# A cross-attention block in float32 on one core: empty instructions in the stream of the matrix engine

## The chip, the cores and the metric

The kernel runs on one core of a Trainium2 chip. The core has five engines that run side by side, each with its own stream of instructions: TensorE (PE, matrix products), VectorE (DVE), ScalarE (ACT), GpSimd (POOL) and SyncE (SP, which here only starts transfers). Engines wait for each other through semaphores. The metric is the device time of one execution in microseconds (us), lower is better.

## The reference

The reference is one block of a transformer with attention from a sequence to a context. `x` and `ctx` are 128 sequences of 128 tokens with 256 features; there are 16 heads of 16 features; all is float32.

```python
q = (x @ Wq + bq);  k = (ctx @ Wk + bk);  v = (ctx @ Wv + bv)     # split into 16 heads
scores = einsum('bhqd,bhkd->bhqk', q, k) / sqrt(16)
scores = where(j < i, scores, -1e30);  attn = softmax(scores);  attn[:, :, 0, :] = 0
x1  = layer_norm(x + (attn @ v) @ Wo + bo, ln1_g, ln1_b)
out = layer_norm(x1 + relu(x1 @ W1 + b1) @ W2 + b2, ln2_g, ln2_b)  # W1: 256 x 1024
```

## The kernel before

The work is cut into 64 pairs of sequences, numbered p = 0 to 63. A pair has 256 tokens. All loops are unrolled in Python: the program has no branch in it, and each engine runs through one long list of instructions from first to last. The order on each engine is the order in which the calls are written, since the kernel asks for a manual schedule. A first part that is written out by hand and the functions `third`, `fourth` and `fifth` bring the pipeline up; `step(p)` for p = 5 to 63 is its steady part; `behind` and the lines from L1200 on empty it.

A step works on several pairs at once. On PE its order is:

1. `weigh(p - 2)` (L461): softmax weights times values, 96 matmuls of 32 columns (L471 and L481).
2. `scores_both(p)` (L347): queries times keys, 64 matmuls on 32 rows by 64 columns (L364).
3. `queries(p + 1)`, `attention_out(p - 2)`, `keys(p + 1)`, `values(p)` (L257, L500, L289): 32 matmuls that stream 256 columns.
4. `second_by_seven(p - 4)` (L771): the second product of the feed-forward part, written as seven products of half size in the manner of Strassen; each `product` (L778) has four matmuls in the program, and the seven go through L780. It starts with step 7.
5. `hidden(p - 3, ...)` (L676): the first product of the feed-forward part, 32 matmuls that stream 256 columns (L687).

A float32 matmul of the program stands in PE's stream as two matmuls with a weight load ahead of each (a transpose as one with one load), so the seven products are 56 matmuls and 56 weight loads. The counts above are those of the stream. A step of the stream holds 280 matmuls and 280 weight loads, and some instructions that only wait for a semaphore (EVENT_SEMAPHORE in the profile).

At the very start PE waits for an identity matrix that POOL makes (`ident`), runs twelve transposes of it whose result nobody reads (L833 to L835), then transposes the first context and input (`ptc` and `ptx`, L224, called from L840), and projects keys and queries (`pk` L859, `pq` L880). Scores, mask, softmax and the first use of the weights follow from these.

The other engines, in a step: DVE adds the mask (L378, L729), finds the maxima (L733, L740), sums the exponentials (L409), turns blocks (L424, L651); ACT computes exponentials (L748) and moves results out of PSUM (L268, L279, L299, L493, L693); POOL divides by the sums (L411) and adds the operands of the seven products (`combine_hidden`, L766 to L769); SP starts the transfers.

Of the kernel before, what the change touches and what calls it, by code (L numbers as in the profile page):

```python
# [13 lines left out]
P = 128  # L14
# [5 lines left out]
def tile_cross_attention_block(  # L20
# [22 lines left out]
    nc = tc.nc  # L43
# [6 lines left out]
    FC = DFF // P  # L50
# [116 lines left out]
    for part in (slice(0, HP), slice(HP, P)):  # L167
        nc.gpsimd.affine_select(
            out=neg[part, 1, :], in_=neg[part, 1, :], compare_op=ALU.is_gt, fill=NEG_INF,
# [10 lines left out]
    for e in range(2):  # L180
        nc.gpsimd.affine_select(
            out=half4[:, e, :], in_=half4[:, e, :], compare_op=ALU.is_ge, fill=0.0,
# [3 lines left out]
            out=half4[:, e, :], in_=half4[:, e, :], compare_op=ALU.is_ge, fill=0.0,  # L186
# [22 lines left out]

    def at_bank(i, name):  # L210
        return psum.tile([P, 512], F32, tag=f"b{i}", name=name)

    def bank(name):
        turns[0] += 1
        return at_bank(4 + turns[0] % 4, name)
# [47 lines left out]
    def queries(p):  # L263
        st = states[p]
        st["qT"] = proj.tile([P, KC, TP], F32, tag="qT", name=f"qT_{p}")
        pq = project(wq, st["xT"], at_bank(4, f"pq_{p}") if p > 3 else bank(f"pq_{p}"))
        for m in range(KC):
            nc.scalar.activation(  # L268
                st["qT"][:, m, :], pq[:, m * TP : (m + 1) * TP], AF.Identity,
                bias=bqs_c[:, m : m + 1], scale=QSCALE,  # L270
            )

    def keys(p):
        st = states[p]
        st["kT"] = proj.tile([P, KC, 2, TP], F32, tag="kT", name=f"kT_{p}")
        pk = project(wk, st["cT"], at_bank(0, f"pk_{p}") if p > 3 else bank(f"pk_{p}"))
        for m in range(KC):
            for e in range(2):
                nc.scalar.activation(  # L279
                    st["kT"][:, m, e, :], pk[:, m * TP : (m + 1) * TP], AF.Identity,  # L280
                    bias=bkh[:, m, e : e + 1], scale=half[:, e : e + 1],
                )
# [467 lines left out]
    wt = const.tile([P, 4, FC // 2, P], F32, tag="wt", name="wt")  # L750
# [20 lines left out]
    def second_by_seven(p):  # L771

        st = states[p]
        hT, hs = st["hT"], st["hS"]
        py = st["py"] = at_bank(6, f"py_{p}")
        pz = st["pz"] = at_bank(7, f"pz_{p}")

        def product(out, left, right):  # L778
            for k in range(FC // 2):
                nc.tensor.matmul(  # L780
                    out, left(k), right(k), start=(k == 0), stop=(k == FC // 2 - 1)
                )

        def raw(e, s):
            return lambda k: hT[:, 2 * k + e, s * P : (s + 1) * P]

        def weights(e, h):
            return lambda k: w2[:, 2 * k + e, h * P : (h + 1) * P]

        product(py[:, :P], raw(0, 0), weights(0, 0))  # L790
        product(pz[:, :P], raw(1, 0), weights(1, 0))
        product(pz[:, 2 * P : 3 * P], raw(1, 1), lambda k: wt[:, 3, k])
        product(py[:, 3 * P :], lambda k: hs[:, 0, k], lambda k: wt[:, 0, k])
        product(py[:, 2 * P : 3 * P], lambda k: hs[:, 2, k], lambda k: wt[:, 2, k])
        product(py[:, P : 2 * P], lambda k: hs[:, 1, k], lambda k: wt[:, 1, k])
        product(pz[:, P : 2 * P], lambda k: hs[:, 3, k], weights(1, 1))

    def sum_of_seven(p):

# [31 lines left out]
        nc.vector.tensor_tensor(st["t2"][:, s], py[:, :D], st["x1b"][:, s], ALU.add)  # L831

    warm = bank("warm")  # L833
    for i in range(12):
        nc.tensor.transpose(warm[:, i % 4 * P : (i % 4 + 1) * P], ident, ident)  # L835
    states[0] = {}
# [271 lines left out]
    def step(p):  # L1108
# [41 lines left out]
        if p > 6:  # L1150
            second_by_seven(p - 4)
        elif p == 6:
            second_half(2, 1)
# [26 lines left out]
    def behind(p):  # L1180

        weigh(p)
        context(p)
        combine_hidden(p - 2, BOTH)
        norm2(p - 3)
        second_by_seven(p - 2)
        attention_out(p)
        attention_sum(p)
        attention_stats(p)
        shift(p, 1)  # L1190
        residual1(p - 1)
        finish(p - 3)
        store(p - 3)
        sum_of_seven(p - 2)
        stats(p - 2, states[p - 2]["t2"], 2)
        scale_and_shift(p - 2)
        hidden(p - 1, range(FC), lambda f: norm1(p) if f == 0 else None)
        turn_x1(p)
# [5 lines left out]
    combine_hidden(p - 1, BOTH)  # L1204
    norm2(p - 2)
    second_by_seven(p - 1)
    residual1(p)
    finish(p - 2)
# [11 lines left out]
    for s in range(2):  # L1220
        py = at_bank(6 + s, f"py_last_{s}")
# [50 lines left out]
```

## Time and profile before

| | us |
|---|---|
| median of 3 runs | 1553.75 |
| lowest, highest | 1552.18, 1554.89 |
| the profiled execution | 1555.99 |
| its span, first to last instruction | 1554.0 |
| PE busy with matmuls in it | 1521.2 |
| PE busy with weight loads in it | 1363.3 |
| DVE, POOL, ACT busy in it | 1327.8, 1265.7, 1120.5 |

The profile is taken by the hardware from one execution. Its page gives the busy time of each engine, the span in slices, the DMA queues, the chain of work that ended last, and groups of instructions. The trace behind it is asked for more: the waits of an engine and what ended them, the instructions in order of time, or the busy time in windows that one chooses. In a row of the timeline stand the start, the length, the engine, the line of the kernel, the operation, the tile written and the tiles read, the shape and the count; in brackets the idle time before it and what ended that. "issue" means that the engine waited for nothing that the profile shows. PEld is the loading of weights, which goes on beside the matmuls. A row "PEldq EVENT_SEMAPHORE" is a wait that PE's sequencer handles; its three numbers are the shortest, the median and the longest in ns.

### The profile page before, as it was taken

The page shows a single profiled execution, that of the slowest core. Times are in us where ns is not written, and L with a number is a line of the kernel's source. Part 1 is how long each engine was busy: PE and PEld are TensorE (multiplying, and loading weights), DVE is VectorE, ACT ScalarE, POOL GpSimd, SP SyncE. Part 2 cuts the span into 40 slices and gives each one's busy share as a digit, 9 for nine tenths or more (in the row PEclk, how much of TensorE's full clock was granted, in tenths as well). Part 3 has the DMA queues.
Part 4 walks back from the last instruction along what each step waited for, and adds up shares of the span by engine and source line. Part 5 has one row for each costly group of instructions (what it writes and reads, how often), then busy time and mean ns, then how long its engine had stood idle before and what let it go on. Part 6 is the DMA issues. An engine that isn't in the chain of part 4 may idle for free.

```text
span 1554.0 us, 47426 instructions
## 1 busy us (share of the span) xinstructions
PE 1521.2 (98%) x17926; PEld 1363.3 (88%) x17926; DVE 1327.8 (85%) x2490; ACT 1120.5 (72%) x3391; POOL 1265.7 (81%) x1290
## 2 busy tenths in 40 slices
PE   8997999999999999999999999999999999999998
PEld 7786989989899889899899899899898899899887
DVE  7987889888889889889889889889889889888854
ACT  5656778777778768778778778678778677777742
POOL 6875888887888888888888888888888888888874
PEclk9999999999999999999999999999999999999999
DMA  8355655555566556556556566556565566554431
GB/s 196 83 120 120 143 134 134 136 132 136 137 138 142 131 134 140 138 134 144 121 138 146 132 140 138 128 136 148 131 139 130 131 138 149 133 136 120 107 91 48
DMA packets 415283, 204.21 MB, mean 131 GB/s; under 512 B 282448, under 2 KB 383056, under 8 KB 415056
## 3 DMA queue, kind: packets, MB, share of 16 engines
q1 hardware_dynamic: 413152, 200.13, 55.7%
q8 instruction: 142, 2.33, 0.7%
q10 hardware_dynamic: 1904, 1.06, 0.3%
q14 instruction: 85, 0.70, 0.1%
HBM read 70.26 MB, written 33.29 MB: 67 GB/s over the span
## 4 chain that ended last, share of the span: by engine, by line
PE 92%; DVE 3%; POOL 3%; issue 1%; ACT 1%; DMA 0%; POOLq 0%; DVEq 0%
PE ph L687 27%; PE py L780 13%; PE pz L780 10%; PE pq L257 8%; PE po L500 7%; PE pv L289 7%; PE pk L257 7%; PE pss L364 6%; PE pc L481 3%; PE pc L471 2%; POOL sm L411 1%; PE py L705 0%; DVE tb L424 0%; DVE sm L378 0%; POOL sd L521 0%
## 5 line engine op out<-in xcount | busy, mean ns | idle before, releaser
L687 PE MATMUL ph<-x1T,w 128*128 128x256 f32 x2048 | 454.0, 379 | 3.0 <-ACT kT L279 3.0
L687 PEld LDWEIGHTS ph<-x1T,w 128*128 128x128 f32 x2048 | 384.6, 190 | 53.9 <-ACT kT L279 3.4
L411 POOL TENSOR_TENSOR sm<-sm,rs 128x1024 f32<-128x1024 f32 x192 | 359.3, 1898 | 7.1 <-ACT hT L693 4.5
L693 ACT ACTIVATE hT<-ph,b1e_c 128x256 f32<-128x256 f32 x504 | 209.8, 468 | 188.3 <-PE ph L687 181.3
L748 ACT ACTIVATE sm<-pss,nmx 128x128 f32<-128x128 f32 x944 | 249.8, 415 | 132.4 <-DVE nmx L733 72.5
L748 ACT ACTIVATE sm<-sm,nmx 128x64 f32<-128x64 f32 x944 | 231.9, 334 | 5.1
L409 DVE TENSOR_REDUCE su<-sm 128x8 f32<-128x1024 f32 (+1 forms) x192 | 225.8, 1176 | 9.4 <-ACT sm L748 5.6
L378 DVE TENSOR_TENSOR sm<-pss,neg 128x256 f32<-128x256 f32 (+1 forms) x276 | 108.0, 433 | 133.0 <-PE pss L364 125.2
L424 DVE STREAM_TRANSPOSE tb<-sm 128x1024 f32<-128x1024 f32 x186 | 220.7, 1213 | 0.0
L520 POOL TENSOR_SCALAR ve<-mv 128x2 f32<-128x2 f32 x127 | 29.7, 234 | 212.4 <-DVE mv L514 212.0
L780 PE MATMUL py<-wt,hS 128*128 128x128 f32 x1440 | 172.0, 276 | 2.9 <-POOL hS L767 2.9
L780 PEld LDWEIGHTS py<-wt,hS 128*128 128x128 f32 x1440 | 166.4, 192 | 3.5 <-POOL hS L767 3.5
L733 DVE TENSOR_REDUCE nmx<-pss 128x4 f32<-128x512 f32 x236 | 150.5, 678 | 0.0
L257 PE MATMUL pq<-xT,wq 128*128 128x256 f32 x504 | 127.3, 396 | 4.9 <-DVE sm L378 4.9
L279 ACT ACTIVATE kT<-pk,bkh,half 128x256 f32<-128x256 f32 x252 | 120.3, 558 | 4.0 <-PE pk L257 4.0
L289 PE MATMUL pv<-wv,cT 128*128 128x256 f32 x512 | 121.1, 379 | 1.6 <-ACT sm L748 1.6
L500 PE MATMUL po<-wo,cxT 128*128 128x256 f32 x512 | 122.4, 382 | 0.0
L257 PE MATMUL pk<-cT,wk 128*128 128x256 f32 x504 | 119.2, 379 | 0.0
L257 PEld LDWEIGHTS pq<-xT,wq 128*128 128x128 f32 x504 | 91.7, 192 | 25.8 <-issue 9.4
L289 PEld LDWEIGHTS pv<-wv,cT 128*128 128x128 f32 x512 | 97.1, 190 | 15.1 <-ACT sm L748 2.0
L500 PEld LDWEIGHTS po<-wo,cxT 128*128 128x128 f32 x512 | 98.0, 192 | 14.0 <-ACT cxT L493 0.3
L257 PEld LDWEIGHTS pk<-cT,wk 128*128 128x128 f32 x504 | 95.7, 190 | 13.1 <-issue 0.2
(131 smaller groups left out, 2973.3 us busy)
## 6 DMA issues: line engine op xcount, KB each, us to landing
pT<-tb SPq DMA_DIRECT2D x984, 96.0 KB
x1t<-tbx SPq DMA_DIRECT2D x252, 64.0 KB
x1T<-x1t SPq DMA_DIRECT2D x63, 256.0 KB
out_dram<-t SPq DMA_DIRECT2D x63, 256.0 KB
xb<-in_x_dram SPq DMA_DIRECT2D x124, 128.0 KB
cb<-in_ctx_dram SPq DMA_DIRECT2D x124, 128.0 KB
x<-in_x_dram SPq DMA_DIRECT2D x31, 512.0 KB
w<-in_L_xattn_W_dram SPq DMA_DIRECT2D x2, 1024.0 KB
```

The source lines that it names most:

```text
L257: nc.tensor.matmul(ps[:, m * TP : (m + 1) * TP], w[:, k, m * P : (m + 1) * P], src[:, k, :], start=(k == 0), stop=(k == KC - 1),)
L279: nc.scalar.activation(st["kT"][:, m, e, :], pk[:, m * TP : (m + 1) * TP], AF.Identity, bias=bkh[:, m, e : e + 1], scale=half[:, e : e + 1],)
L289: nc.tensor.matmul(pv[:, s * D : (s + 1) * D], st["cT"][:, k, s * P : (s + 1) * P], wv[:, k, :], start=(k == 0), stop=(k == KC - 1),)
L409: nc.vector.tensor_reduce(su, sm[:, part, :], AX.X, ALU.add)
L411: nc.gpsimd.tensor_tensor(sm[:, part, :], sm[:, part, :], rs[:, :, None].to_broadcast([P, part.stop - part.start, n]), ALU.mult,)
L424: nc.vector.transpose(st["tb"][:, :, at : at + 256].rearrange("p j (n a) -> p n j a", a=32), st["sm", hi].rearrange("p h j -> p (h j)")[:, ...
L500: nc.tensor.matmul(po[:, s * D : (s + 1) * D], cxT[:, k, s, :], wo[:, k, :], start=(k == 0), stop=(k == KC - 1),)
L687: nc.tensor.matmul(ph[:, i * TP : (i + 1) * TP].rearrange("p (s i a) -> p s i a", s=2, a=32), w1[:, k, (f + i) * P : (f + i + 1) * P], st[ ...
L693: nc.scalar.activation(st["hT"][:, f + i, :], ph[:, i * TP : (i + 1) * TP], AF.Relu, bias=(b1e_c if p else b1_c)[:, f + i : f + i + 1], sc ...
L733: nc.vector.tensor_reduce(st["nmx", 1][:, 4 * r : 4 * r + 4], st["sps", 1][r].rearrange("p (n j) -> p n j", j=P), AX.X, ALU.max, negate=True,)
L748: nc.scalar.activation(sm[:, h, :], src, AF.Exp, bias=nmx[:, h : h + 1], scale=1.0)
L780: nc.tensor.matmul(out, left(k), right(k), start=(k == 0), stop=(k == FC // 2 - 1))
```

## The change

A new function puts empty instructions into PE's stream; they read nothing, write nothing and wait for nothing. In `second_by_seven`, each of the seven products gets one, behind its first matmul (`1 // 4 + (1 % 4 > k)` is one for k = 0 and none for k = 1 to 3). With these seven a step has 576 instructions on PE. 44 more stand at the start, ahead of the twelve transposes of `ident`. The seven products run 60 times (57 in the steps from p = 7 on, three while the pipeline empties), so 464 empty instructions are added. No other engine's list changes.

```diff
+    def empty(n):
+        for _ in range(n):
+            nc.tensor.nop(hint="pad", nofuse=True)
+
...
-        def product(out, left, right):
+        def product(out, left, right, after):
             for k in range(FC // 2):
                 nc.tensor.matmul(
                     out, left(k), right(k), start=(k == 0), stop=(k == FC // 2 - 1)
                 )
+                empty(after // (FC // 2) + (after % (FC // 2) > k))
...
-        product(py[:, :P], raw(0, 0), weights(0, 0))
+        product(py[:, :P], raw(0, 0), weights(0, 0), 1)
...
     warm = bank("warm")
+    empty(44)
     for i in range(12):
         nc.tensor.transpose(warm[:, i % 4 * P : (i % 4 + 1) * P], ident, ident)
```

The six other calls of `product` get the same last argument, 1.

More of the change, by code (lines that the diff above doesn't have):

```diff
@@ L788, in weights @@
             return lambda k: w2[:, 2 * k + e, h * P : (h + 1) * P]
-        product(py[:, :P], raw(0, 0), weights(0, 0))
[L791 to L796, printed above, removed]
+        product(py[:, :P], raw(0, 0), weights(0, 0), 1)
+        product(pz[:, :P], raw(1, 0), weights(1, 0), 1)
+        product(pz[:, 2 * P : 3 * P], raw(1, 1), lambda k: wt[:, 3, k], 1)
+        product(py[:, 3 * P :], lambda k: hs[:, 0, k], lambda k: wt[:, 0, k], 1)
+        product(py[:, 2 * P : 3 * P], lambda k: hs[:, 2, k], lambda k: wt[:, 2, k], 1)
+        product(py[:, P : 2 * P], lambda k: hs[:, 1, k], lambda k: wt[:, 1, k], 1)
+        product(pz[:, P : 2 * P], lambda k: hs[:, 3, k], weights(1, 1), 1)
     def sum_of_seven(p):
```

## The prediction

> **What bounds the kernel now.** I read the head of the page first, then the list of waits of TensorE (PE) alone, then windows cut at the starts of steps, then the timeline of PE around the few steps that stick out.
>
> ```profile
> span 1554.0 us, 47426 instructions
> PE 1521.2 (98%) x17926; PEld 1363.3 (88%) x17926; DVE 1327.8 (85%) x2490; ACT 1120.5 (72%) x3391; POOL 1265.7 (81%) x1290
> q8 instruction: 142, 2.33, 0.7%
> ```
>
> PE is busy for 98% of the span, so only its gaps and the pace of its stream count. The third line is a DMA queue that carries no data: 142 packets, 2.33 MB, 16.4 KB each. PE's stream has 17,926 matmuls, as many weight loads, and its semaphore waits. These five rows are the waits of one step (320 to 343 us), and they add up to nine:
>
> ```profile
> L364 PEldq EVENT_SEMAPHORE  x2: 51/51/51, 320.7 to 320.8; - x2
> L471 PEldq EVENT_SEMAPHORE  x4: 51/51/51, 338.9 to 339.2; - x4
> L257 PEldq EVENT_SEMAPHORE  x1: 51/51/51, 323.9 to 323.9; - x1
> L289 PEldq EVENT_SEMAPHORE  x1: 51/51/51, 325.2 to 325.2; - x1
> L687 PEldq EVENT_SEMAPHORE  x1: 51/51/51, 333.9 to 333.9; - x1
> ```
>
> A step is thus 280 matmuls + 280 weight loads + 9 = 569 instructions. The whole stream is 2 x 17,926 + about 570 = 36,420, and 36,420 / 142 = 256.5: I read a packet as one block of 256 PE instructions.
>
> Now the steps (start:end, length, then PE busy, PEld, DVE, ACT, POOL, clock and DMA). The first six stand out; the other five are ordinary.
>
> ```profile
> 342.85:367.85 25.00, 23.67 (x281) 21.20 (x280) 20.85 (x40) 17.85 (x55) 20.87 (x24) 1.00 0.62 146
> 554.18:578.47 24.29, 23.67 (x281) 21.20 (x280) 20.81 (x40) 17.85 (x55) 19.96 (x22) 1.00 0.55 125
> 764.87:789.45 24.58, 23.67 (x281) 21.20 (x281) 20.81 (x40) 17.85 (x55) 20.57 (x22) 1.00 0.62 146
> 975.79:999.80 24.01, 23.68 (x281) 21.20 (x281) 20.83 (x40) 17.85 (x55) 20.01 (x22) 1.00 0.57 126
> 1186.13:1210.72 24.59, 23.68 (x282) 21.18 (x281) 20.81 (x40) 17.85 (x55) 20.55 (x22) 1.00 0.62 144
> 1397.05:1421.06 24.01, 23.68 (x282) 21.18 (x281) 20.81 (x40) 17.86 (x55) 20.04 (x22) 1.00 0.42 105
> ...
> 226.40:249.69 23.29, 23.29 (x281) 21.07 (x281) 20.65 (x40) 17.74 (x55) 19.62 (x20) 1.00 0.57 129
> 249.69:272.98 23.29, 23.29 (x281) 21.07 (x281) 20.66 (x40) 17.73 (x55) 19.63 (x20) 1.00 0.64 148
> 367.85:391.14 23.29, 23.29 (x281) 21.07 (x280) 20.49 (x39) 17.74 (x55) 18.42 (x17) 1.00 0.53 118
> 437.72:461.01 23.29, 23.29 (x281) 21.07 (x280) 20.66 (x40) 17.73 (x55) 19.62 (x20) 1.00 0.63 149
> 1303.88:1327.17 23.29, 23.29 (x281) 21.07 (x280) 20.65 (x40) 17.73 (x55) 19.62 (x20) 1.00 0.56 127
> ```
>
> An ordinary step takes 23.29 us and PE is busy in all of it. The six long ones start nine steps apart: 554.18 - 342.85 = 211.33 = 25.00 + 8 x 23.29. Their excess is 1.71 + 1.00 + 1.29 + 0.72 + 1.30 + 0.72 = 6.74 us. Nine steps are 9 x 569 = 5121 = 20 x 256 + 1 instructions, so after nine steps the blocks begin at the same places, one instruction earlier. That period is what makes me put the excess down to the blocks. The timeline of the first long step, with an ordinary one (319.56) ahead of it, shows the place:
>
> ```profile
> 319.56 0.43 PE L471 MATMUL pc<-pT,vd 128*32 128x64 f32 x16
> ...
> 321.04 1.62 PE L364 MATMUL pss<-kT,qT 32*64 32x128 f32 x64
> 322.59 0.70 PE L257 MATMUL pq<-xT,wq 128*128 128x256 f32 x2
> ```
> ```profile
> 344.33 1.57 PE L364 MATMUL pss<-kT,qT 32*64 32x128 f32 x61
> 347.23 0.43 PE L364 MATMUL pss<-kT,qT 32*64 32x128 f32 x3 [1.33 <-issue]
> ```
>
> PE stops between the 61st and the 62nd of the 64 score matmuls, and waits for nothing that the profile knows ("issue"). I count positions in PE's stream from the step's first weight load (`weigh`, L471). `weigh` has 96 matmuls, so the stop is at 2 x (96 + 61) + 2 waits = 316: a block begins there, and the one before it began at 60. The DMA view of 344.2 to 344.4 us has this row:
>
> ```profile
> q8 instruction: 1, 0.02, 46.4%
> ```
>
> One block's packet starts there, 1.4 to 1.6 us into the step, and takes 46.4% of 16 x 0.2 = 1.48 us. PE resumes 1.3 to 1.5 us after its end. So I read the stop as PE running out of instructions: the block from 316 on is asked for only after the block from 60 on has been begun, and is usable by 347.23, 4.4 us into the step. Positions 0 to 322, `weigh` and the scores, take PE only 322.59 - 319.56 = 3.03 us; the other 247 take 20.26 us. Only there can 256 instructions be used up faster than the next block arrives.
>
> **The change part by part.** Nothing moves; PE gets 44 + 60 x 7 empty instructions, and the list of the changed kernel's instructions holds them all: 44 at the head, and one behind the first matmul of each of the seven products of L780.
>
> *Where the blocks begin.* In the present kernel the place shifts by 569 - 512 = 57 per step, modulo 256. From 60 in the step at 342.85 this gives 89 at 226.40, 32 at 249.69, 3 at 367.85, 88 at 437.72 and 27 at 1303.88, all 23.29 us long. The six long steps have 60 down to 55, so every row that I have puts the trouble between 32 and 84. In the changed kernel the step that was at 342.85 (p = 15) has 44 ahead and 8 x 7 from steps 7 to 14, so its blocks begin 100 earlier: 60 - 100 = -40, that is 216. From there the shift is 576 - 512 = 64 per step, and the places repeat every four steps: 24, 88, 152, 216. 88 is the place of the step at 437.72, which does not stop. 24 lies between 3 and 27, which do not. 152 and 216 need their next block at 408 and 472, far behind position 322. So all six stops go: **-6.74 us**. Behind them comes nothing that was waiting its turn: in an ordinary step PE is busy for 23.29 of 23.29 us, and this pace stays.
>
> The list of PE's waits has seven stops of this kind, one more than the six long steps. The timeline shows it at 129.90.
>
> ```profile
> PE pss L364 <- issue: 5.4, 7, 1.3
> ```
> ```profile
> 129.90 1.29 PE L364 MATMUL pss<-kT,qT 32*64 32x128 f32 x43 [0.94 <-issue]
> 136.10 1.22 PE L257 MATMUL pq<-xT,wq 128*128 128x256 f32 x2 [4.91 <-DVE sm L378]
> ```
>
> This seventh (0.94 us) counts for nothing, because PE soon idles 4.91 us for the mask on DVE whatever it did before.
>
> *The seven of each step.* No empty instruction is in the trace. The nearest row is the semaphore wait, which PE's sequencer also handles alone: 51 ns, and four of them in a row began from 338.9 to 339.2 us, 0.1 us apart. Those four stand ahead of the `weigh` of 342.85, so the sequencer is 3.6 us ahead of the array there. One empty instruction every 17, at 0.05 to 0.1 us, is covered by this lead: **0**. Without the cover it would be 60 x 7 x 0.05 = 21 to 42 us. [...]
>
> *The 44 at the head.* They stand behind the barrier's wait and ahead of the first transposes:
>
> ```profile
> L1253 PEldq EVENT_SEMAPHORE  x1: 51/51/51, 0.7 to 0.7; - x1
> 1.44 2.82 PE L835 MATMUL warm<-ident 128*128 128x128 f32 x12 [1.44 <-POOL ident masks.py:199]
> 4.68 1.07 PE L224 MATMUL ptc<-ident,c_first 128*128 128x128 f32 x4 [0.41 <-DMA c_first<-in_ctx_dram]
> 5.59 0.60 PE L224 MATMUL ptx<-ident,x 128*128 128x128 f32 x4
> ```
>
> At nothing each they hide in the wait for `ident`. At 51 ns they take 2.24 us and end at about 3.0; the twelve transposes begin 1.57 us late, 0.41 of it is covered by the wait for `c_first`, and the products begin **1.2 us** late. At 0.1 us they end at 5.2, and the products are 3.3 us late. The early transposes run 0.21 us apart and `ptx` 0.11; if that change of pace comes later too, up to 0.4 us is added. All that follows up to the first softmax hangs on these products, so I count the delay in full. I take 51 ns, the row's own duration, since an empty instruction has nothing to test. [...]
>
> Sum: 1554.0 - 6.74 + 1.2 = 1548.5 us of span. The profiled execution took 1555.99, 2.2 us over the median of 1553.75; the same -5.5 on the median gives **1548.2 us**. Bounds of the unknown: -6.7 (1547.0) to -6.7 + 3.7 (1550.8).
>
> **Rivals.**
> *Fetching is hidden.* The packets arrive in time, the stops have another cause, and shifting blocks moves nothing. Then only the head's 1.2 us is left: 1555. Against it speak the nine-step period and the packet that overlaps the stop. [...]
>
> *The places are wrong (slower).* If 24 or 88 is inside the region after all, because the arrival of a block scatters, every fourth step stops: 14 stops at the mean of 6.74 / 6 = 1.12 us are 15.7 us, and 1548.2 + 15.7 = 1564. It decides from one stop in every 11 steps on, where it eats the gain. For it: the repeat after four steps makes a bad place permanent, while now it drifts away. Against it: 88, 27 and 3 are in rows above.
>
> *An empty instruction holds the array (slower).* If PE empties its queue for each, a weight load that now lies beside a matmul is exposed.
>
> ```profile
> L780 PEld LDWEIGHTS py<-wt,hS 128*128 128x128 f32 x1440 | 166.4, 192 | 3.5 <-POOL hS L767 3.5
> ```
>
> At 192 ns, 420 of them cost 81 us, at 51 ns 21 us: 1569 to 1629. It decides from 13 ns each on. Against it: waits are just as foreign to the array, nine stand in each step, and PE is busy throughout.
>
> *The head costs more.* At 0.1 us each or above, the gain falls to 3 us or less: 1551 to 1553.
>
> **How the numbers follow.** What a measurement of this kernel can tell from no change is about 0.2%, 3.1 us. Forecast 0.66 (faster); dear head 0.14 and hidden fetching 0.05 (within 0.2%); wrong places 0.08 and held array 0.07 (slower). So faster 0.66, same 0.19, slower 0.15. The range goes from 1546.0, the free head less 1 us for the scatter of the runs (1552.18 to 1554.89), to 1553.0, the end of the dear head: 0.66 + 0.14 = 0.80. The forecast's own range is 1546.0 to 1550.8.
>
> **What would show it.** Right: windows cut at step starts all 23.29 us, PE's waits without "pss <- issue" behind 170 us, `ptc` at about 5.8 us, everything else as now. Wrong: long steps four apart (places); ordinary steps above 23.29 (held array); `ptc` at 7 or later (head); long steps still nine apart or at random (another cause).

## The result, and the profile after

| | kernel before | changed kernel | ratio, 95% interval |
|---|---|---|---|
| first comparison, median of 17 runs each | 1553.9 | 1550.99 | 0.9979 (0.9972 to 0.9986) |
| lowest, highest | 1551.95, 1556.4 | 1548.3, 1552.71 | |
| again, on another chip, medians of 27 and 11 runs | 1556.01 | 1550.69 | 0.9970 (0.9959 to 0.9982) |
| the profiled executions | 1555.99 | 1548.3 | |

The changed kernel is faster, by 0.21% in the first comparison and by 0.30% in the second. The forecast was 1548.2 us; the time is 2.8 us above it. It is inside the range, but 0.2 us above the end of the forecast's own part of it (1550.8), where the part of the dear head begins. The profiled execution of the changed kernel is the lowest of its 17 runs, and that of the kernel before lies above the median of its own, so the two traces show a larger difference (span 1554.0 to 1546.2, 7.8 us) than the medians do. I therefore read the traces piece by piece, and take the time from the medians.

The head of the page of the changed kernel:

```profile
span 1546.2 us, 47890 instructions
PE 1518.6 (98%) x17926; PEld 1362.5 (88%) x17926; DVE 1329.0 (86%) x2490; ACT 1119.8 (72%) x3391; POOL 1265.3 (82%) x1290
q8 instruction: 144, 2.36, 0.7%
```

There are 464 more instructions, and 144 packets of 256 instructions in place of 142: 464 / 256 = 1.8. The matmuls are the same 17,926. The three longest waits of PE:

```profile
PE pq L261 <- DVE sm L382: 5.2, 1, 5.2
PE warm L841 <- POOL half L185: 4.1, 1, 4.1
PE py L784 <- POOL hS L771: 3.1, 3, 1.9
```

The row "pss <- issue", 5.4 us in seven stops before, is gone from the whole list. The wait ahead of the transposes of `ident` has grown from 1.44 to 4.1 us. Windows cut at the starts of six steps (columns as before):

```profile
343.61:366.90 23.29, 23.29 (x282) 21.07 (x281) 20.65 (x40) 17.74 (x55) 19.64 (x20) 1.00 0.63 148
390.19:413.48 23.29, 23.29 (x282) 21.07 (x281) 20.66 (x40) 17.73 (x55) 19.63 (x20) 1.00 0.63 149
413.48:436.77 23.29, 23.29 (x281) 21.07 (x281) 20.66 (x40) 17.73 (x55) 19.62 (x20) 1.00 0.56 125
553.23:576.52 23.29, 23.29 (x282) 21.07 (x281) 20.34 (x39) 17.73 (x55) 19.63 (x20) 1.00 0.56 126
762.85:786.14 23.29, 23.29 (x282) 21.07 (x281) 20.66 (x40) 17.73 (x55) 19.63 (x20) 1.00 0.62 148
1391.70:1414.99 23.29, 23.29 (x281) 21.07 (x280) 20.66 (x40) 17.73 (x55) 19.64 (x20) 1.00 0.43 111
```

The first, fourth, fifth and last are steps that were long before (342.85, 554.18, 764.87 and 1397.05). All take 23.29 us, with seven empty instructions in each. For the whole steady part I compare the starts of `weigh` in the first step with the seven products (p = 7) and in the last step (p = 63), first in the kernel before, then in the changed one:

```profile
156.52 0.43 PE L471 MATMUL pc<-pT,vd 128*32 128x64 f32 x16
...
1467.64 0.43 PE L471 MATMUL pc<-pT,vd 128*32 128x64 f32 x16
```
```profile
157.28 0.43 PE L475 MATMUL pc<-pT,vd 128*32 128x64 f32 x16
...
1461.58 0.43 PE L475 MATMUL pc<-pT,vd 128*32 128x64 f32 x16
```

Before, the 56 steps take 1467.64 - 156.52 = 1311.12 us; now 1461.58 - 157.28 = 1304.30, which is 23.29 for each. The steady part has given 6.82 us. What was lost is at the start (timeline of PE in the changed kernel):

```profile
4.10 2.79 PE L841 MATMUL warm<-ident 128*128 128x128 f32 x12 [4.10 <-POOL half L185]
6.69 1.06 PE L228 MATMUL ptc<-ident,c_first 128*128 128x128 f32 x4
```
```profile
L215 PEldq NOP  x464: 13/13/13, 0.9 to 1525.1; - x155
```

The transposes begin at 4.10 in place of 1.44, and `ptc` at 6.69 in place of 4.68, 2.0 us late. The name in the bracket is only the last semaphore event that the profile found; what PE was doing were the 44 empty instructions, which start from 0.9 to 4.0 us. Each is recorded with 13 ns, but from the first at 0.9 to the transposes at 4.10 they take 3.2 us, **73 ns each**. The duration in such a row isn't the distance between two of them.

So the two terms that I can name are -6.8 and +2.0, -4.8 together. Of the other 3.0 of the 7.8 us between these two traces, 1.7 lie behind the last `weigh` (1554.0 - 1467.64 = 86.3 to 1546.2 - 1461.58 = 84.7), and 1.2 between the head and the step p = 7, which is 0.76 us late and not 2.0. In both places the clock of PE falls to 0.50 for 3.4 or 6.8 us at a time, in one trace or in both, and not for the same stretches in the two (last section). The part behind the last `weigh` differs by as much without any change: an unaltered run of the kernel before (`before_2`) has 84.8 us there. An unaltered second run of the changed kernel (`after_2`) has the step p = 7 at 158.32, 1.8 us late, and a span of 1548.7, 5.3 under that of before.

### The profile page after: what moved, and what is told of

Same layout as the page of the kernel before. It is cut to its first block, busy times and chain, and to the rows that moved or that the text cites. A ratio compares the mean times of both kernels' runs of the same rounds, so it can differ in the third digit from the quotient of the medians.

```text
span 1546.2 us, 47890 instructions
## 1 busy us (share of the span) xinstructions
PE 1518.6 (98%) x17926; PEld 1362.5 (88%) x17926; DVE 1329.0 (86%) x2490; ACT 1119.8 (72%) x3391; POOL 1265.3 (82%) x1290
## 3 DMA queue, kind: packets, MB, share of 16 engines
q10 hardware_dynamic: 1904, 1.06, 0.3%
## 4 chain that ended last, share of the span: by engine, by line
PE 92%; POOL 3%; DVE 3%; issue 1%; ACT 1%; DMA 0%; POOLq 0%; DVEq 0%
PE ph L691 27%; PE py L784 13%; PE pz L784 10%; PE pq L261 8%; PE po L504 7%; PE pk L261 7%; PE pv L293 7%; PE pss L368 6%; PE pc L485 3%; PE pc L475 2%; POOL sm L415 1%; PE py L709 0%; DVE tb L428 0%; DVE sm L382 0%; POOL sd L525 0%
```

## The experiments

My theory: PE stops where a block begins at a place from which the next 256 instructions are used up before the next block is there; only as far as the end of the score matmuls is PE that fast (322 instructions in 3.03 us, then 247 in 20.26), so only some places stop, and the seven per step keep the blocks on four good places. The first rival: the empty instructions cost something where they stand, and the stops have another reason. The second: any other number of instructions would have done as well.

Positions are those of the prediction: instructions from the step's first weight load. An empty instruction ahead moves the place where a block begins one position earlier. "Excess" is a step's length less 23.29 us, and "steady excess" the time from the `weigh` of p = 7 to that of p = 63, less the 1304.30 us that the changed kernel takes for it. Times are medians. The kernels of each of the three parts ran on one chip, with its own runs of the kernel before: 1555.82, 1556.01 and 1555.77 us.

### The two parts alone, and the head moved or shortened

**`head_only`**: the 44 at the head, none in the steps.

```diff
-                empty(after // (FC // 2) + (after % (FC // 2) > k))
```

> Only the 44 empty instructions at the head; the steps keep 569 instructions. Theory (PE runs dry where a block of 256 begins between about 35 and 80): the blocks still wander, their places are 44 earlier, so one family comes by at 44 down to 39 and one at 73 down to 68, and never at 60 to 55. Both are at the rim, so the stops are short: 0 to 0.5 us each, 0 to 3 us in all, against 6.7 us before. The head costs 2.1 us (products begin at 6.7 us and not 4.7). Time 2 to 4 us under before. Rival (the stops hang on the drift alone, not on the place): six or seven stops of about 1.1 us as before, so 2 us over before.

Measured: 1558.87 against 1555.82, ratio 1.0018 (1.0009 to 1.0027). The places drift as before, 44 positions earlier:

```profile
230.33:255.02 24.69, 23.88 (x281) 21.20 (x280) 20.83 (x40) 17.88 (x55) 20.58 (x23) 1.00 0.57 127
...
441.66:466.43 24.77, 23.89 (x281) 21.21 (x281) 20.83 (x40) 17.89 (x55) 20.67 (x23) 1.00 0.62 146
...
1377.29:1401.35 24.06, 23.56 (x281) 21.06 (x281) 20.84 (x40) 17.89 (x55) 20.03 (x22) 1.00 0.62 144
```

The first two begin a block at 45 and 44 and exceed by 1.40 and 1.48 us, the third at 68, by 0.77. The steady excess is 6.5 us, as large as before. I had expected at most 3: I took 44 for a place at the rim and left 45 out, and the two stop as hard as 55 to 60, while 43 to 41 cost 0.2 to 0.5 us each and 73 to 68 cost 0.3 to 0.8. With a head that costs 2 us or more nothing is gained (the step p = 7 begins at 160.46 us, 3.9 late). The rival's figure for the time was the nearer one; its picture wasn't, since no step outside these places exceeds by more than 0.05 us.

**`steps_only`**: seven per step, nothing at the head.

```diff
     warm = bank("warm")
-    empty(44)
```

> Only the seven empty instructions in each step, none at the head. The blocks then begin at 4, 68, 132 and 196, the same every four steps. Theory: no cost at the head; if 68 is still inside the place where PE runs dry, every fourth step stops for 0.2 to 0.6 us, 3 to 8 us in all, and the time is between 4 us under before and 1 us over it; if 68 is outside, no stop is left and it is 6.7 us under before. Rival (the seven instructions themselves cost time in the steps): ordinary steps above 23.29 us.

Measured: 1560.06, ratio 1.0033 (1.0021 to 1.0045). The places now repeat every four steps, 44 positions later than in the changed kernel: 4, 68, 132, 196.

```profile
414.29:438.69 24.40, 23.55 (x281) 21.06 (x280) 20.83 (x40) 17.88 (x55) 20.40 (x22) 1.00 0.57 126
508.56:532.93 24.37, 23.56 (x282) 21.07 (x281) 20.92 (x40) 17.89 (x55) 20.23 (x22) 1.00 0.57 132
...
1167.22:1190.64 23.42, 23.42 (x281) 21.06 (x281) 20.79 (x40) 17.87 (x55) 19.64 (x20) 1.00 0.56 126
```

These three are steps with place 68. Fourteen of them exceed by 0.13 to 1.16 us, 11.6 in all, more than the six stops of the kernel before, and more than the 0.2 to 0.6 us each that I had expected at 68; the steps between them take 23.29 us. So the same seven per step make the kernel slower without the 44.

**`head_behind`**: the 44 moved behind the twelve transposes of `ident`. The places in the steps are those of the changed kernel.

```diff
-    empty(44)
     for i in range(12):
         nc.tensor.transpose(warm[:, i % 4 * P : (i % 4 + 1) * P], ident, ident)
+    empty(44)
```

> The changed kernel with the 44 empty instructions behind the twelve transposes of ident instead of ahead of them. From there on every instruction has the same place in its block as in the changed kernel. Theory: 44 x 0.071 us = 3.1 us now run while the array does the transposes (2.8 us) and waits for c_first until 4.7 us, so the first products begin at 4.7 to 5 us instead of 6.7, and the time is 2 us under the changed kernel, about 1549. Rival (the head is not what keeps the timed gain at 2.9 us): the same time as the changed kernel, 1551.

Measured: 1548.15, ratio 0.9952 (0.9940 to 0.9964): 7.7 us under the kernel before. The head costs nothing there (timeline of its start):

```profile
1.44 2.82 PE L840 MATMUL warm<-ident 128*128 128x128 f32 x12 [1.44 <-POOL ident masks.py:199]
4.72 0.63 PE L228 MATMUL ptc<-ident,c_first 128*128 128x128 f32 x4 [0.45 <-DMA c_first<-in_ctx_dram]
```

The transposes begin at 1.44 and `ptc` at 4.72, within 0.04 us of the kernel before. PE's sequencer hands out the 44 (from 1.5 to 4.6 us) while the array works on the transposes. The steady excess is -0.1 us.

**`head_8`**: eight at the head in place of 44, so that the places are 36 positions later: 60, 124, 188, 252.

```diff
-    empty(44)
+    empty(8)
```

> The changed kernel with 8 instead of 44 empty instructions at the head, which puts a block's beginning at 60 in every fourth step. Theory: each of these 14 steps stops for 1 to 1.7 us at the scores, 14 to 24 us in all; the head is hidden (0.6 us in the wait for ident). Time 7 to 17 us over before. Rival (only the repeat matters, not the place): no stops, 6.7 us under before.

Measured: 1565.62, ratio 1.0068 (1.0056 to 1.0080), 9.8 us over the kernel before. Here the prediction's rival of the wrong places can be seen:

```profile
415.01:439.37 24.36, 23.66 (x281) 21.19 (x280) 20.82 (x40) 17.88 (x55) 20.36 (x22) 1.00 0.56 126
439.37:462.66 23.29, 23.29 (x281) 21.07 (x280) 20.49 (x39) 17.76 (x55) 18.94 (x19) 1.00 0.61 143
509.24:533.72 24.48, 23.67 (x282) 21.20 (x281) 20.93 (x40) 17.88 (x55) 20.34 (x22) 1.00 0.56 126
603.59:628.20 24.61, 23.67 (x282) 21.20 (x281) 20.83 (x40) 17.88 (x55) 20.56 (x22) 1.00 0.56 126
```

The long steps start four steps apart (509.24 - 415.01 = 94.23 = 24.36 + 3 x 23.29), and the step between is ordinary. Fourteen stops give a steady excess of 18.7 us, 1.34 each. This kernel has 36 instructions fewer than the changed one, all of them ahead of the first product, and by the ratios (1.0068 to 0.9970 and 0.9979) it is some 14 to 15 us slower.

### The changed kernel again, the moved head again, a longer head, ten times as many

**`after_2`** is the changed kernel unaltered.

> The changed kernel once more, unaltered, beside the version with the 44 behind the transposes, on one chip. The steady steps give 6.8 us and the products begin 2 us late, which leaves 4.7, but 2.9 were timed. Theory (the late head costs more than its 2 us, because the granted clock then falls in other stretches of the start): in this trace the steady steps are 23.29 us again, and step 7 (the sixth weigh) begins 2 to 4 us later than in the kernel before. Rival (the seven instructions of the steps cost 2 us that the first trace happened not to show): steps over 23.29 us.

Measured: 1550.69, ratio 0.9970 (0.9959 to 0.9982). Steady excess 0.0, so the rival is out. The step p = 7 begins 1.8 us later than in the kernel before, just short of the 2 to 4 that I had expected.

**`behind_2`** is `head_behind` unaltered.

> The version with the 44 behind the transposes, unaltered, on the chip of the run beside it. Theory: 2 to 4 us under the changed kernel and 6 to 8 us under the kernel before. Rival (the first comparison came from another chip): the same time as the changed kernel.

Measured: 1549.38, ratio 0.9962 (0.9951 to 0.9973). It is 1.3 us under `after_2` on the same chip, less than the 2 to 4 that I had expected; the two intervals overlap, so by times alone this difference isn't shown. The trace shows the earlier start: `ptc` at 4.74 against 6.69, the step p = 7 at 155.77 against 158.32.

**`head_108`**: 64 more at the head, which gives the same four places.

```diff
-    empty(44)
+    empty(108)
```

> The changed kernel with 108 empty instructions at the head: 64 more, which leaves every later place in a block the same but for one step's shift. Theory: 64 x 0.071 = 4.5 us later, all of it on the path, so 4 to 6 us over the changed kernel. Rival (the head is covered by the first load and softmax): no more than 1 us over it.

Measured: 1557.13, ratio 1.0014 (1.0005 to 1.0023), 6.4 us over `after_2`. The timeline of its start:

```profile
8.76 2.79 PE L841 MATMUL warm<-ident 128*128 128x128 f32 x12 [8.76 <-issue]
11.34 1.06 PE L228 MATMUL ptc<-ident,c_first 128*128 128x128 f32 x4
```

64 more move the transposes from 4.10 to 8.76: 4.66 / 64 = 73 ns each, the same as for the first 44. `ptc` moves by 4.65 us, so the head is on the path in full; the other 1.8 of the 6.4 are not accounted for by it. Some 1.3 of them lie ahead of the step p = 7, which begins 6.0 us later than in `after_2`. No step is long (steady excess 0.0).

**`steps_71`**: `head_behind` with 71 empty instructions per step in place of seven. A step then has 640, two and a half blocks, and the places are 216 and 88 in turn.

```diff
-        product(py[:, :P], raw(0, 0), weights(0, 0), 1)
+        product(py[:, :P], raw(0, 0), weights(0, 0), 10)
...
-        product(pz[:, P : 2 * P], lambda k: hs[:, 3, k], weights(1, 1), 1)
+        product(pz[:, P : 2 * P], lambda k: hs[:, 3, k], weights(1, 1), 11)
```

> The version with the 44 behind the transposes, and ten times the empty instructions in each step: 71, ten or eleven for each of the seven products. Blocks begin at 88 and 216 only. Theory (the sequencer runs 3.6 us ahead, and 71 x 0.071 = 5.0 us are spread over 6.2 us of products): steps of 23.29 us, the same time as with seven, 6 to 8 us under before. Rival (they cost what they take): 64 x 0.071 x 60 = 270 us more.

Measured: 1548.83, ratio 0.9959 (0.9946 to 0.9973). Two neighbouring kinds of step:

```profile
342.69:365.98 23.29, 23.29 (x281) 21.07 (x281) 20.66 (x40) 17.73 (x55) 19.63 (x20) 1.00 0.62 148
389.27:412.56 23.29, 23.29 (x281) 21.07 (x280) 20.66 (x40) 17.73 (x55) 19.63 (x20) 1.00 0.61 142
```

71 per step cost as little as seven. At the 73 ns measured at the head they would be 5.2 us of the sequencer's time in each step, which is an estimate; none of it reaches the array, since the steps stay at 23.29 us.

### The kernel before again, and the lower rim

**`before_2`** and **`before_3`** are the kernel before, unaltered, one execution each.

> The kernel before, unaltered, for a second trace. Theory (the stops are block arrivals, so their places are fixed by the program and their lengths are not): long steps at the same six places, 60 down to 55, with other lengths, 4 to 9 us in all. Rival (the six long steps were an accident of one execution): other steps, or none.

> The kernel before, unaltered, for a third trace. Theory: again the same six steps, with a sum that differs from the first trace's 6.7 us by 1 to 3 us, which is part of why the kernel before was timed at 1553.9 in one comparison and at 1556.0 in another. Rival: the same sum to 0.2 us, so that the difference lies elsewhere.

Measured: 1556.49 and 1556.29. Two of the six long steps of `before_2`, and the sum over the six of `before_3`:

```profile
342.97:368.24 25.27, 23.67 (x281) 21.20 (x280) 21.02 (x40) 17.88 (x55) 20.86 (x24) 1.00 0.62 144
554.56:579.45 24.89, 23.68 (x282) 21.20 (x281) 20.82 (x40) 17.88 (x55) 20.54 (x22) 1.00 0.56 124
```
```profile
sum 146.82, PE 142.06 PEld 127.17 DVE 124.92 ACT 107.12 POOL 122.26; mean PE 23.68 PEld 21.20 DVE 20.82 ACT 17.85 POOL 20.38
```

The same six steps stop in all three traces. How long they stop differs: 342.85 took 25.00 in the first trace and its counterpart here 25.27, and the six sum up to 6.7, 8.8 and 146.82 - 6 x 23.29 = 7.1 us. So what the change removes is 6.7 to 8.8 us, run by run. The difference of 1 to 3 us that I expected is there in `before_2` and not in `before_3`.

**`behind_28`**: `head_behind` with 28, so that the places are 40, 104, 168, 232.

```diff
-    empty(44)
+    empty(28)
```

> 28 instead of 44 empty instructions behind the transposes, which puts a block's beginning at 40 and 104 in every four steps. Theory: 40 is the lower rim (stops of 0.2 to 0.5 us were seen at 41 to 43, none at 32): 14 stops of 0 to 0.3 us, so 0 to 4 us over the version with 44. Rival (the region reaches below 40): 14 stops of 1 us or more, 14 us over it.

Measured: 1549.47, ratio 0.9960 (0.9945 to 0.9975). Two of its steps with place 40:

```profile
224.98:248.94 23.96, 23.90 (x282) 21.22 (x281) 20.83 (x40) 17.89 (x55) 19.97 (x22) 1.00 0.56 126
412.36:435.65 23.29, 23.29 (x282) 21.07 (x281) 20.65 (x40) 17.77 (x55) 19.66 (x20) 1.00 0.56 125
```

The same place exceeds by 0.67 us once and by nothing another time; six of the fourteen steps with place 40 stop, for 0.13 to 0.72 us, 2.5 us in all. So 40 is at the lower rim.

These fourteen steps also show what a stop waits for. In each, one packet of 256 instructions starts between 0.4 us before the step and 0.4 us after its start. The DMA views of 225.2 to 225.3 and of 411.9 to 412.0 us have those of the two steps above:

```profile
q8 instruction: 1, 0.02, 89.6%
```
```profile
q8 instruction: 1, 0.02, 82.2%
```

They take 89.6% and 82.2% of 16 x 0.1 us, 1.43 and 1.32 us. So the first ends about 1.7 us after its step's start and that step stops; the second ends 0.9 us after its own, and that step doesn't. In the trace, all eight steps without a stop have their packet's end 0.65 to 1.06 us after the step's start, and the six that stop have it at 1.05 (0.17 us of excess), 1.33 (0.13), 1.44 (0.39), 1.48 (0.45), 1.66 (0.66) and 1.89 (0.72). The program and the place are the same in all of them; what differs is when the packet ends. The places 55 to 60 agree: in the 14 long steps of `head_8` and the 18 in the three traces of the kernel before, PE goes on 1.1 to 1.6 us after that packet's end.

All kernels in one table (the first place is that of the step p = 15, the others those of p = 18, 17 and 16, and so on every four steps; for `steps_71`, p = 15 and 16; "drift" means by one position in nine steps):

| kernel | places | steady excess, us | time | over its kernel before |
|---|---|---|---|---|
| before | drift, stops at 60 to 55 | 6.8, 8.7, 7.1 | 1553.9 to 1556.0 | |
| changed, `after_2` | 216, 24, 88, 152 | 0.0, 0.0 | 1550.99, 1550.69 | -2.9, -5.3 |
| `head_only` | drift, stops at 45 to 41, 73 to 68 | 6.5 | 1558.87 | +3.1 |
| `steps_only` | 4, 68, 132, 196 | 11.6 | 1560.06 | +4.2 |
| `head_8` | 252, 60, 124, 188 | 18.7 | 1565.62 | +9.8 |
| `behind_28` | 232, 40, 104, 168 | 2.6 | 1549.47 | -6.3 |
| `head_behind`, `behind_2` | 216, 24, 88, 152 | -0.1, 0.0 | 1548.15, 1549.38 | -7.7, -6.6 |
| `steps_71` | 216, 88 | 0.0 | 1548.83 | -7.2 |
| `head_108` | 152, 216, 24, 88 | 0.0 | 1557.13 | +1.1 |

## Why the prediction was right, and where it was not

**The stops go: right, in mechanism and size.** Predicted -6.74 us, measured -6.82 in the steady part. That these are so close is no test of the size, since both take the stops from the same trace of the kernel before; with those of `before_2` it would be 8.7. `head_8` and `steps_only` show that it is the place that decides: the same seven per step give 18.7, 11.6 or 0.0 us of excess with 8, 0 or 44 ahead. Adding 64 ahead (`head_108`), or 64 in each step (`steps_71`), leaves the places among the same four and stops nothing. The prediction put the trouble "between 32 and 84" (84 is the place of the step at 1280.59 us, p = 55, 23.29 us long, which it doesn't show). The runs have stops from 40 to 73; no step stood at 33 to 39 or at 74 to 83, so the exact rims aren't known. The nearest of the four places, 24 and 88, stand some 15 positions off.

The runs show the place and the period of 256 by changing them. That the cause is the arrival of the next block is shown by `behind_28`, where the place stays and the stop follows the end of the block's packet. No run set the time of an arrival by itself; why one packet starts earlier or takes longer than another stays open. Steps with the places 24, 88, 152 and 216 take 23.29 us; at places from 40 to 73 they take up to 25.27 us.

**The seven of each step cost nothing: right.** Steps take 23.29 us with none, seven and 71. The rival of the held array, 21 us or more, is refuted. The traces list the empty instructions with PE's sequencer (PEldq NOP, 13 ns each: 464 in the changed kernel, 4304 in `steps_71`).

**The 44 at the head: the term that was mis-sized.** The prediction took 51 ns from the semaphore waits, 2.24 us, and products 1.2 us late. The trace shows 73 ns, 3.2 us, and `ptc` 2.0 us late, at 6.69 in place of "about 5.8"; the bound of 0.1 us each had held it. The row that I chose gave a recorded duration, and what counts is the distance from one to the next: the four waits quoted beside it were 0.1 us apart, an empty instruction is recorded with 13 ns and stands 73 apart. With 2.0 in place of 1.2 the sum is 1553.75 - 6.74 + 2.0 = 1549.0. How much of the 2.0 us is left at the step p = 7 differs from trace to trace: 0.76 us in the first of the changed kernel, 1.8 in `after_2` and 3.9 in `head_only`, each against the first trace of the kernel before.

**"This seventh counts for nothing": shown.** `pq`, which waits for the mask on DVE behind it, begins at 136.10 in the kernel before, with a stop of 0.94 us ahead of it. In `steps_71`, where nothing stops there:

```profile
128.19 2.24 PE L368 MATMUL pss<-kT,qT 32*64 32x128 f32 x64
136.03 3.78 PE L261 MATMUL pq<-xT,wq 128*128 128x256 f32 x8 [5.59 <-DVE sm L382]
```

The score matmuls begin at 128.19 (128.27 before), and `pq` at 136.03. In `head_8` the stop at this place is 1.35 us, and `pq` begins at 136.07. So 0, 0.94 and 1.35 us of stop end at the same time.

**The rest, and what stays open.** The first comparison's gain, 2.9 us, is little over half of the 5.5 us that were forecast, and its time lies in the range only because the range takes in the dear head. The dear head itself (0.1 us or more each) is not what the trace shows, so that the range held is in part luck. 1549.0 is 2 us under the first median and 1.7 under the second. The second comparison gave -5.3 us between medians (-2.8 to -6.4 by its interval), which holds the -4.8 of the two terms; the first gave -2.9 (-2.2 to -4.4), less than -4.8. The changed kernel took 1551 on both chips, but the kernel before 1553.9 on the first and 1555.8 to 1556.0 on the three others. Its stops do vary between traces (6.7 to 8.8 us), and so does the clock at both ends; which of them makes the first chip 2 us quicker with it wasn't tried.

**Better than both** is `head_behind`: the same places, with the 44 where PE's array has work. It took 1548.15 and 1549.38, 6.6 to 7.7 us under the kernel before; over the changed kernel the trace shows a start of the products that is 2 us earlier, while the times alone (1.3 us on one chip) do not yet separate the two.

## What to carry to other kernels

Where an engine that is busy throughout has a few long repeats of one step, at a period that the work doesn't have, look for what is counted in instructions: here blocks of 256, which stopped PE only where it is quickest through its instructions (322 in 3.03 us; blocks that begin at places from 40 to 73). A step length with a short period modulo 256 freezes the places, for good or ill, so the number ahead has to be chosen with it: 36 instructions too few made this kernel some 14 to 15 us slower. Put such filling where the array has work in hand, since 71 per step were free there and 44 ahead of the first product cost 2 us.

## What was not expected of the hardware

In these two traces PE's granted clock falls to half for 3.4 or 6.8 us at a time at the start and in the tail, and the same program doesn't always get the same stretches. Windows of the kernel before, then of the changed one, with the clock in the third column from the end:

```profile
1531.30:1534.70 3.40, 3.40 (x17) 3.34 (x16) 1.70 (x4) 0.00 (x0) 3.32 (x3) 0.51 0.27 80
26.10:29.50 3.40, 2.94 (x14) 2.98 (x15) 3.29 (x5) 1.64 (x4) 3.27 (x3) 0.50 1.24 265
135.30:142.10 6.80, 6.00 (x14) 4.79 (x15) 6.48 (x14) 4.29 (x17) 2.65 (x5) 0.50 0.62 149
```
```profile
1525.00:1528.40 3.40, 3.40 (x25) 3.13 (x24) 2.18 (x5) 0.00 (x0) 3.32 (x4) 1.00 0.28 82
28.80:32.20 3.40, 3.40 (x24) 3.07 (x30) 2.59 (x4) 1.91 (x4) 3.27 (x3) 0.50 1.02 135
120.90:127.70 6.80, 6.10 (x14) 4.88 (x15) 2.04 (x3) 6.76 (x26) 2.30 (x2) 0.50 0.89 177
```

In the tail PE waits for `hS` on POOL in both, and then runs the same matmuls:

```profile
1530.11 2.69 PE L780 MATMUL py<-wt,hS 128*128 128x128 f32 x16 [1.87 <-POOL hS L767]
1532.59 1.91 PE L780 MATMUL pz<-w,hS 128*128 128x128 f32 x8
```
```profile
1523.87 2.05 PE L784 MATMUL py<-wt,hS 128*128 128x128 f32 x16 [1.89 <-POOL hS L771]
1525.76 1.06 PE L784 MATMUL pz<-w,hS 128*128 128x128 f32 x8
```

After a gap of 1.87 us the clock was 0.51 and `pz` took 1.91 us; after one of 1.89 us it was 1.00 and 1.06 us. In `after_2`, the same program as the changed kernel, it was 0.50 again from 1526.3 to 1529.7. So this differs from one execution to the next and isn't the change's. From the last `weigh` on, the three traces take 86.3, 84.7 and 86.1 us; `before_2`, where the clock doesn't fall there, takes 84.8. Ahead of the step p = 7, the kernel before has 6.8 us at half clock from 135.3 on; the changed one has 6.8 us from 120.9 and 3.4 us from 138.0. In `after_2` the stretch of 6.8 us begins at 137.1, 1.8 us later than in the kernel before, and the step p = 7 is 1.8 us late too. That the 1.2 us there come from the clock is argued from these times, not shown. Why the clock fell after the gap of 1.87 us and not after that of 1.89 us isn't shown.
